# Turning a grouped convolution's results on VectorE instead of TensorE, with a new partition order of its input

## The chip, the core and the metric

The kernel runs on one core of one Trainium2 chip. The core has a matrix engine (TensorE, PE in the profile), a vector engine (VectorE, DVE), a scalar engine (ScalarE, ACT), GpSimd (POOL) and SyncE (SP). They run their own instruction streams and wait for each other by semaphores. A transfer is started by an instruction in the stream of one of the engines and is carried out by the core's 16 DMA engines. In this kernel nearly all transfers are started from SP.

The metric is the device time of one execution in microseconds. Before the change the median of three runs is 2969.51 us (2966.65 to 2975.18).

## What is computed

The input is 32 images of 14 x 14 pixels with 512 channels, float32. Two residual layers follow each other, each behind a group norm over 32 groups of 16 channels (`_gn`):

```python
def _L0_conv_ref(x, block_w, block_b, fc1_w, fc1_b, fc2_w, fc2_b, gammas):
    anchors = []
    for i in range(NUM_BLOCKS):                       # 18
        nx = gelu(einsum('bhwc,cd->bhwd', x, block_w[i]) + block_b[i])
        if i in TARGET_IDX:                           # 11, 14, 17
            t = TARGET_IDX.index(i)
            pooled = nx.mean(axis=(1, 2))
            h = gelu(pooled @ fc1_w[t] + fc1_b[t])
            logits = (h @ fc2_w[t] + fc2_b[t]).reshape(-1, A, C)
            gates = softmax(logits, axis=1)
            routed = einsum('bac,bahwc->bhwc', gates, stack(anchors))
            nx = nx + gammas[t] * routed
        x = nx
        if i in ANCHOR_IDX:                           # 1, 4, 9
            anchors.append(x)
    return x

def _L1_conv_ref(x, W):                               # 3 x 3, SAME, 32 groups
    return conv_general_dilated(x, W, ..., feature_group_count=32)

x = x + _L0_conv_ref(_gn(x), ...)
x = x + _L1_conv_ref(_gn(x), W)
```

The change concerns the second line, the 3 x 3 convolution in groups of 16 channels, and, on a small scale, how the input of the first one is brought in.

## The kernel before

**Blocks.** Channels lie on the 128 partitions, in four chunks, and pixels along the free dimension. A tile holds two images (392 pixels); sixteen tiles form eight pairs. One of the 18 blocks on a pair is a *step*: a 512 x 512 matrix product with seven half-size products instead of eight (`block`, L412; the products are line 431, the subtractions ahead of a step `pre_adds`, line 410, ScalarE saves intermediate results in line 464, VectorE adds in line 468, and the gelu is line 444 or 451). A product is a *tick*, so that a step has seven ticks. The steps of neighbouring pairs are interleaved in an order written out by hand, and ahead of step 15 of the last pair stands a *gap*, a step without products, in which other work of TensorE is put.

**The planner.** All other work is put at ticks. `at(tick, f)` places a call; `put(first, need, f)` places it at the first tick from `first` on at which VectorE ("dve") or ScalarE ("act") has `need` microseconds left of a budget (`ROOM`, by the tick's number within the step; `TAIL` behind the last step, `tend`); `hold` takes some of a budget away. `block` calls `run(tick)` behind each product, and that is the order in which the engines' streams, SP's too, receive their instructions. The streams are in order: a transfer whose buffer isn't free holds up everything that SP has behind it.

**Start of a pair.** `plan_start` begins LEAD ticks ahead of a pair's first step. `load_blocks` fetches 32 x 12 x 32 blocks of the transposed input (`xb`, line 256, from four SP instructions per tile and chunk) and the remaining eight pixels' part of all four chunks (`xr`), and VectorE turns them in 32 x 32 blocks (`turn_blocks`, lines 274 and 276). NIN = 4 such buffers are in use at a time.

**Gates.** After blocks 11, 14 and 17 the weights of the gate are loaded (line 517 for the first layer), then `gate_hidden` (`hps`, line 547), `gate_logits` (`lps`, line 563), a softmax, and the weighted sum of the anchors by VectorE and ScalarE (`gate_part`, `gate_add` in line 643, `gate_last`, `gate_base` in line 611). Behind the last block GpSimd adds the input to the result (`residual`, a transfer that accumulates).

**From layer one to layer two.** `plan_norm` computes the group norm's statistics, and `columns` writes the sum and its normed form into `xc` (lines 721, 731, 733) and from there to DRAM, in `x2d` (line 740). A row of `x2d` is one image column of one channel; columns 0 to 7 and 6 to 13 are the two halves `v` (KC = 8 columns each, of which SO = 7 are results), index `e` tells the plain sum from its normed form, and the last index runs over 8 images x 14 rows, NV = 112.

**Convolution.** Two pairs form a batch of eight images (NBAT = 4). A batch has 16 *units* of two groups of 16 channels each; four units (UC) make up one chunk of 128 channels. The partitions of a unit are the 16 channels and 8 columns of a group, so that the taps along a row become three 128 x 128 band matrices, one for each of the three rows of the filter. They are built once by VectorE (`load_taps`, `build_band`, lines 828 and 835, with `mask`), stored in DRAM and fetched again for each unit or kept. A unit goes through four calls:

1. `unit_load`: one SP instruction (line 858) brings both groups' rows, 448 KB; where the bands aren't kept another one (line 866) brings them.
2. `unit_taps`: twelve matmul instructions (line 879) into PSUM.
3. `unit_sum`: VectorE adds the result to the plain sum, in place (line 889).
4. `unit_out`: four transposes on TensorE (line 903, `tpo`) put images and rows on the partitions; two ScalarE copies (line 908) put them into the output tile `o` of 112 x 14 x 128; after the chunk's fourth unit ScalarE starts one output transfer of 784 KB (line 913).

`plan_unit` places these: the load some ticks ahead, no earlier than the unit five places back (NX = 5 buffers) has gone out; then the sum with 0.65 us of VectorE and `unit_out` with 0.9 us of ScalarE. Batches 0 and 1 have their 16 units beside the blocks of later pairs. Of batch 2 four units stand ahead of the gap, NGAP = 6 in the gap, and NLATE = 6 behind the last step (`tend`), where they fill TensorE while the last pair's gate and norm are computed. The 16 units of batch 3 come last of all, chunk by chunk as the norm's results arrive.

Of the kernel before, what the change touches and what calls it, by code (L numbers as in the profile page):

```python
# [19 lines left out]
def kernel(  # L20
# [53 lines left out]
    inpool = ctx.enter_context(tc.tile_pool(name="inpool", bufs=4))  # L74
# [59 lines left out]
    def run(tick):  # L134
# [23 lines left out]
        mask[:, 1 : GP + 1], ident.rearrange("p (i k) -> p k i", k=GP), AX.X, ALU.add  # L158
# [92 lines left out]
    def load_blocks(t, c):  # L251
# [8 lines left out]
        if c == 0:  # L260
            xr = d["xr"] = inpool.tile([P, NCK, TB], F32, tag="xr", name=f"xr_{t}", bufs=2)
            for q in range(P // TB):
                nc.sync.dma_start(xr[q * TB : (q + 1) * TB], cols[q, N - TB :])

    def turn_blocks(t, c):
# [9 lines left out]
        if cc == NH - 1:  # L275
            nc.vector.transpose(xq[:, :, N - TB :], d["xr"][:, h * NH : (h + 1) * NH])
            nc.sync.dma_start(xkeep[t][h], xq.rearrange("p c n -> p (c n)"))
# [60 lines left out]
    def plan_start(p):  # L338
# [3 lines left out]
        NIN = 4  # L342
# [4 lines left out]
        for j, (t, c) in enumerate(parts):  # L347
            at(t0 - LEAD - 8 if j < NIN else turned[j - NIN], load_blocks, t, c)
            turned.append(put(max(a, turned[j - NIN] + 5 if j >= NIN else 0), {"dve": 0.45 + c % NH * 0.15}, turn_blocks, t, c))
# [457 lines left out]
    def load_taps(c):  # L807
# [3 lines left out]
        for i in range(CG):  # L811
            nc.sync.dma_start(
                tw[i * KC : (i + 1) * KC], src[i].partition_broadcast(KC)
            )
# [4 lines left out]
    def build_band(g, dx):  # L819
# [3 lines left out]
        shape = [P, 3, CG, KC]  # L823
        if dx == 0:
# [5 lines left out]
            tw[:, :, dx, gl * CG : (gl + 1) * CG].unsqueeze(3).to_broadcast(shape),  # L830
            mask[:, dx : dx + KC].unsqueeze(1).unsqueeze(1).to_broadcast(shape),
# [4 lines left out]
        if dx == 2:  # L836
            nc.sync.dma_start(band[g // 2][:, g % 2], t[0].rearrange("p y o k -> p (y o k)"))
            del built[g]
# [15 lines left out]
    def unit_load(m, u):  # L854
# [3 lines left out]
        nc.sync.dma_start(  # L858
            xs.rearrange("r g e n -> r g (e n)"),
            x2d[m][c].rearrange("(g r) e v n -> r g (e v n)", r=P)[:, 2 * ul : 2 * ul + 2],  # L860
        )
# [30 lines left out]

    def unit_out(m, u):

        d = units.pop((m, u))
        c, ul = divmod(u, UC)
        if ul == 0:
            outs[m] = outpool.tile([NV, W, P], F32, tag="o", name=f"o_{m}_{c}")
        tp = aux(f"tpo_{m}_{u}")
        for g in range(2):  # L900
            for v in range(2):
                j = v * 2 + g
                nc.tensor.transpose(  # L903
                    tp[:NV, j * P : (j + 1) * P], d["xs"][:, g, 0, v * NV : (v + 1) * NV], ident
# [183 lines left out]
```

## Time and profile before

| | |
|---|---|
| median of the three runs | 2969.51 us |
| the profiled execution's own time | 2968.65 us |
| span of its profile, from the first to the last instruction | 2966.6 us |
| granted TensorE clock | 0.994 |
| matmuls of line 431, x<-t,s alone (the largest of its groups) | 2304 x 494 ns |
| transposes of results, tpo, line 903 | 256 instructions, 38.8 us busy |
| copies of them, line 908 on ScalarE | 128 x 348 ns, 37.8 us busy |
| sums, line 889 on VectorE | 64 x 616 ns, 39.3 us busy |
| bytes moved by transfers that SP starts (q1) | 448.79 MB |
| bytes moved by those that ScalarE starts (q10) | 13.65 MB |
| mean rate of all transfers over the span | 161 GB/s |

An instruction's mean is the time from its start to its end; TensorE overlaps successive instructions, so that the busy time of a group of matmuls is less than count times mean (256 transposes of 274 ns are 38.8 us busy, 152 ns each). "Busy" of an engine is the share of the span in which it executed something, and says nothing of who waited for whom. For that the page has the chain that ended last: from the last instruction back, at each step, to what released it, or to the instruction before it on its engine. A group's "idle before" is how long its engine stood idle just ahead of these instructions, with what ended most of that. SPq is SyncE's own sequencer, that is, the instructions that start transfers; the time of such an instruction is the time that SP is held, not that of the transfer.

The page also divides the span into 40 slices of 74 us. TensorE is 90% busy or more in all but the first and the last (8 and 6 tenths), its granted clock is at nine tenths or more in all but the last (8), and the transfers' share of the 16 DMA engines' time, between 3 and 7 tenths up to there, is 8 and 9 tenths in the last two slices.

### The profile page before, as it was taken

The page shows a single profiled execution, that of the slowest core. Times are in us where ns is not written, and L with a number is a line of the kernel's source. Part 1 is how long each engine was busy: PE and PEld are TensorE (multiplying, and loading weights), DVE is VectorE, ACT ScalarE, POOL GpSimd, SP SyncE. Part 2 cuts the span into 40 slices and gives each one's busy share as a digit, 9 for nine tenths or more (in the row PEclk, how much of TensorE's full clock was granted, in tenths as well). Part 3 has the DMA queues.
Part 4 walks back from the last instruction along what each step waited for, and adds up shares of the span by engine and source line. Part 5 has one row for each costly group of instructions (what it writes and reads, how often), then busy time and mean ns, then how long its engine had stood idle before and what let it go on. Part 6 is the DMA issues. An engine that isn't in the chain of part 4 may idle for free.

```text
span 2966.6 us, 31628 instructions
## 1 busy us (share of the span) xinstructions
PE 2926.8 (99%) x9889; PEld 1795.7 (61%) x9889; DVE 1764.8 (59%) x3393; ACT 1430.9 (48%) x3355; POOL 78.1 (3%) x60
## 2 busy tenths in 40 slices
PE   8999999999999999999999999999999999999996
PEld 5555555555556566666666666666666665656666
DVE  5887787755377454763547635576455753545663
ACT  4435445545455444554444544445445454544561
POOL 0000000000000000000000000000000000000010
PEclk9999999999999999999999999999999999999998
DMA  5554446733475346654566544665446653343689
GB/s 160 163 181 138 164 145 174 202 114 117 149 198 158 130 135 175 205 164 130 166 164 182 172 135 154 173 175 168 140 154 165 182 159 125 122 136 118 205 224 212
DMA packets 483017, 477.31 MB, mean 161 GB/s; under 512 B 247987, under 2 KB 310562, under 8 KB 482850
## 3 DMA queue, kind: packets, MB, share of 16 engines
q1 hardware_dynamic: 452450, 448.79, 49.4%
q0 software_dynamic: 4608, 12.85, 2.4%
q10 hardware_dynamic: 25792, 13.65, 1.8%
q8 instruction: 80, 1.31, 0.2%
q14 instruction: 87, 0.71, 0.1%
HBM read 393.41 MB, written 93.03 MB: 164 GB/s over the span
## 4 chain that ended last, share of the span: by engine, by line
PE 96%; DVE 1%; DMA 1%; SPq 1%; issue 0%; ACT 0%; DVEq 0%
PE x L431 50%; PE z L431 25%; PE y L431 13%; PE cps L879 5%; PE lps L563 1%; PE tpo L903 1%; PE hps L547 1%; SPq L740 0%; SPq L256 0%; SPq L851 0%; DMA x<-x2d 0%; PE warm L991 0%; DMA w<-in_L_conv_block_w_dram 0%; DMA xin<-in_x_dram 0%; DMA x2d<-xc 0%
## 5 line engine op out<-in xcount | busy, mean ns | idle before, releaser
L431 PE MATMUL x<-t,s 128*128 128x392 f32 x2304 | 809.6, 494 | 0.1
L444 ACT ACTIVATE o<-c,bias 128x392 f32<-128x392 f32 x720 | 440.3, 620 | 666.2 <-DVE c L468 662.5
L431 PEld LDWEIGHTS x<-t,s 128*128 128x128 f32 x2304 | 433.5, 190 | 301.9 <-issue 0.2
L468 DVE TENSOR_TENSOR c<-x,c 128x392 f32<-128x392 f32 x288 | 160.5, 565 | 491.3 <-PE x L431 417.3
L464 ACT COPY c<-x 128x392 f32<-128x392 f32 x576 | 278.2, 483 | 352.9 <-PE x L431 347.6
L431 PE MATMUL x<-t,w 128*128 128x392 f32 x1152 | 402.8, 492 | 1.0 <-DVE c L468 1.0
L431 PE MATMUL z<-t,s 128*128 128x392 f32 x1152 | 402.9, 492 | 0.0
L431 PE MATMUL y<-o,w 128*128 128x392 f32 x1088 | 380.9, 493 | 0.2 <-ACT o L444 0.2
L431 PE MATMUL z<-o,s 128*128 128x392 f32 x1088 | 380.6, 492 | 0.0
L431 PE MATMUL x<-o,w 128*128 128x392 f32 x1088 | 380.4, 492 | 0.0
L468 DVE TENSOR_TENSOR c<-y,c 128x392 f32<-128x392 f32 x288 | 162.4, 564 | 276.3 <-PE y L431 198.0
L431 PEld LDWEIGHTS x<-t,w 128*128 128x128 f32 x1152 | 218.8, 190 | 161.7 <-DVE c L468 1.6
L431 PEld LDWEIGHTS z<-t,s 128*128 128x128 f32 x1152 | 217.6, 190 | 154.5 <-DMA s<-skeep 0.3
L410 DVE TENSOR_TENSOR t<-o,o 128x784 f32<-128x784 f32 x272 | 264.0, 971 | 65.4 <-ACT o L444 63.5
L431 PEld LDWEIGHTS z<-o,s 128*128 128x128 f32 x1088 | 206.0, 190 | 148.9
L431 PEld LDWEIGHTS x<-o,w 128*128 128x128 f32 x1088 | 206.4, 190 | 147.8 <-DMA w<-in_L_conv_block_w_dram 0.7
L431 PEld LDWEIGHTS y<-o,w 128*128 128x128 f32 x1088 | 205.0, 190 | 146.2 <-ACT o L444 1.0
L410 DVE TENSOR_TENSOR t<-o,t 128x784 f32<-128x784 f32 x272 | 264.3, 972 | 4.7
L464 ACT COPY c<-z 128x392 f32<-128x392 f32 x288 | 139.2, 483 | 211.0 <-PE z L431 210.9
L468 DVE TENSOR_TENSOR c<-z,c 128x392 f32<-128x392 f32 x288 | 158.9, 563 | 109.7 <-PE z L431 108.5
L451 ACT ACTIVATE o<-c,bias 128x196 f32<-128x196 f32 x288 | 129.4, 450 | 91.3 <-DVE c L468 90.5
L444 ACT ACTIVATE o<-x,bias 128x392 f32<-128x392 f32 x240 | 137.3, 581 | 71.5 <-PE x L431 65.2
(109 smaller groups left out, 2014.3 us busy)
## 6 DMA issues: line engine op xcount, KB each, us to landing
w<-in_L_conv_block_w_dram SPq DMA_DIRECT2D x144, 1024.0 KB
s<-skeep SPq DMA_DIRECT2D x504, 256.0 KB
x2d<-xc SPq DMA_DIRECT2D x128, 224.0 KB
x<-x2d SPq DMA_DIRECT2D x64, 448.0 KB
skeep<-s SPq DMA_DIRECT2D x72, 256.0 KB
bw<-band SPq DMA_DIRECT2D x38, 384.0 KB
xkeep<-xt SPq DMA_DIRECT2D x32, 392.0 KB
o<-xkeep POOLq DMA_DIRECT2D x32, 392.0 KB, 7.4
```

Of the source, the lines that this page charges most:

```text
L410: nc.vector.tensor_tensor(t[j], i0, i1, ALU.subtract)
L431: nc.tensor.matmul(acc[d][:, :N], lhsT=lhsT[:, kk, d * P : (d + 1) * P], rhs=rhs[:, kk, :], start=first and kk == 0, stop=kk == NH - 1, sk ...
L444: nc.scalar.activation(o[:, d, :], srcs[d], AF.Gelu_apprx_tanh, bias=bias[:, r : r + 1])
L451: nc.scalar.activation(o[:, d, sl], srcs[d][:, sl], AF.Gelu_apprx_tanh, bias=bias[:, r : r + 1], accum_out=pooled[:, c, m : m + 1],)
L464: nc.scalar.copy(cs[d], acc[d][:, :N])
L468: nc.vector.tensor_tensor(cs[d], acc[d][:, :N], cs[d], ALU.add)
L547: nc.tensor.matmul(hps[:, :NB4], lhsT=w1[:, kk, :], rhs=box["pooled"][:, kk, :], start=(kk == 0), stop=(kk == NCK - 1),)
L563: nc.tensor.matmul(lps[:, m * NB4 : (m + 1) * NB4], lhsT=w2[:, m * P : (m + 1) * P], rhs=h, start=True, stop=True,)
L879: nc.tensor.matmul(pv[:, :, lo:hi], lhsT=d["bw"][:, g, dy], rhs=xv[:, :, lo + dy - 1 : hi + dy - 1], start=j == 0, stop=j == 2, skip_group ...
L903: nc.tensor.transpose(tp[:NV, j * P : (j + 1) * P], d["xs"][:, g, 0, v * NV : (v + 1) * NV], ident)
```

## The change

Input, bands and output of the convolution take another order, and with it another engine turns the results:

- **Partition order.** The partitions of a unit are (column, channel) instead of (channel, column): in `mask`, in the bands (`build_band`), and in `unit_load`, whose source is now rearranged. That takes two transfers of one group each in place of one of two. `x2d` itself stays as it was. `load_taps` fills its tile with eight transfers of 16 partitions instead of sixteen of 8.
- **Turning.** `unit_out` has two VectorE transposes in 32 x 32 blocks, one for each group, in place of four on TensorE and two copies on ScalarE. 32 partitions are two columns of 16 channels. A block takes 28 (TR) of the 112 positions and 4 more, which belong to the next block and aren't used; 8 blocks (of both halves) make up a group, 256 elements a partition. The output tile `o` has 32 positions x 4 pairs of columns on its partitions.
- **Output.** After the chunk's fourth unit 14 transfers go out, one for each image column, of 28 x 4 rows of 128 channels, started by SP; before, it was one, started by ScalarE.
- **Planner.** `unit_out` books 0.6 us of VectorE, possibly at the tick of the sum, and nothing of ScalarE; the budgets held for the units in the gap and behind the last step change accordingly. NGAP is 5 and NLATE 7, where they were 6 and 6.
- **Start of a pair.** `inpool` has three buffers instead of four, and NIN is 3; the remainder `xr` is loaded for two chunks at a time instead of four; LEAD is 42 instead of 35, the first loads start 6 ticks ahead of the turning instead of 8, and a later block is turned 4 ticks or more behind its load instead of 5.

```diff
--- before.py
+++ after.py
@@ -71,7 +71,7 @@
     fpool = ctx.enter_context(tc.tile_pool(name="fpool", bufs=1))
     qpool = ctx.enter_context(tc.tile_pool(name="qpool", bufs=38))
     tmp = ctx.enter_context(tc.tile_pool(name="tmp", bufs=6))
-    inpool = ctx.enter_context(tc.tile_pool(name="inpool", bufs=4))
+    inpool = ctx.enter_context(tc.tile_pool(name="inpool", bufs=3))
     outpool = ctx.enter_context(tc.tile_pool(name="outpool", bufs=2))
     cvpool = ctx.enter_context(tc.tile_pool(name="cvpool", bufs=2))
     small = ctx.enter_context(tc.tile_pool(name="small", bufs=2))
@@ -155,7 +155,7 @@
     mask = const.tile([P, GP + 2], F32, name="mask")
     nc.vector.memset(mask, 0.0)
     nc.vector.tensor_reduce(
-        mask[:, 1 : GP + 1], ident.rearrange("p (i k) -> p k i", k=GP), AX.X, ALU.add
+        mask[:, 1 : GP + 1], ident.rearrange("p (k i) -> p k i", k=GP), AX.X, ALU.add
     )
 
     mhalf = const.tile([P, NR], F32, name="mhalf")
@@ -257,10 +257,10 @@
                 xs[q * TB : (q + 1) * TB],
                 cols[q, : NTB * TB, c].rearrange("(n j) i -> j n i", j=TB),
             )
-        if c == 0:
-            xr = d["xr"] = inpool.tile([P, NCK, TB], F32, tag="xr", name=f"xr_{t}", bufs=2)
+        if c % NH == 0:
+            xr = d["xr", c // NH] = inpool.tile([P, NH, TB], F32, tag="xr", name=f"xr_{t}_{c}", bufs=2)
             for q in range(P // TB):
-                nc.sync.dma_start(xr[q * TB : (q + 1) * TB], cols[q, N - TB :])
+                nc.sync.dma_start(xr[q * TB : (q + 1) * TB], cols[q, N - TB :, c : c + NH])
 
     def turn_blocks(t, c):
         d = starts[t]
@@ -273,7 +273,7 @@
         xq = d["xq"][h]
         nc.vector.transpose(xq[:, cc, : NTB * TB], xs.rearrange("p n i -> p (n i)"))
         if cc == NH - 1:
-            nc.vector.transpose(xq[:, :, N - TB :], d["xr"][:, h * NH : (h + 1) * NH])
+            nc.vector.transpose(xq[:, :, N - TB :], d.pop(("xr", h)))
             nc.sync.dma_start(xkeep[t][h], xq.rearrange("p c n -> p (c n)"))
 
     xkeep = [
@@ -339,14 +339,14 @@
 
         t0 = NP7 * at_step[p, 0]
         parts = [(2 * p + n, c) for n in range(2) for c in range(NCK)]
-        NIN = 4
+        NIN = 3
         a = t0 - LEAD
         at(a - 30, copy_in, p)
         turned = []
         b = 0
         for j, (t, c) in enumerate(parts):
-            at(t0 - LEAD - 8 if j < NIN else turned[j - NIN], load_blocks, t, c)
-            turned.append(put(max(a, turned[j - NIN] + 5 if j >= NIN else 0), {"dve": 0.45 + c % NH * 0.15}, turn_blocks, t, c))
+            at(t0 - LEAD - 6 if j < NIN else turned[j - NIN], load_blocks, t, c)
+            turned.append(put(max(a, turned[j - NIN] + 4 if j >= NIN else 0), {"dve": 0.45 + c % NH * 0.15}, turn_blocks, t, c))
             a = turned[j]
         for j, (t, c) in enumerate(parts):
             b = max(b, put(turned[j // NH * NH + NH - 1], {"dve": 0.7}, stats_in, t, c))
@@ -808,10 +808,8 @@
 
         tw = outpool.tile([P, NTAP, P], F32, tag="o", name=f"tw_{c}")
         src = conv_w.rearrange("kh kw i d -> i (kh kw) d")[:, :, c * P : (c + 1) * P]
-        for i in range(CG):
-            nc.sync.dma_start(
-                tw[i * KC : (i + 1) * KC], src[i].partition_broadcast(KC)
-            )
+        for k in range(KC):
+            nc.sync.dma_start(tw[k * CG : (k + 1) * CG], src)
         taps[c] = tw
 
     built = {}
@@ -820,21 +818,21 @@
 
         tw = taps[g // GP].rearrange("p (y x) d -> p y x d", x=3)
         gl = g % GP
-        shape = [P, 3, CG, KC]
+        shape = [P, 3, KC, CG]
         if dx == 0:
             built[g] = cvpool.tile([P, 2] + shape[1:], F32, tag="x", name=f"bt_{g}", bufs=NX)
         t = [built[g][:, v] for v in range(2)]
         o = t[min(dx, 1)]
         nc.vector.tensor_tensor(
             o,
-            tw[:, :, dx, gl * CG : (gl + 1) * CG].unsqueeze(3).to_broadcast(shape),
-            mask[:, dx : dx + KC].unsqueeze(1).unsqueeze(1).to_broadcast(shape),
+            tw[:, :, dx, gl * CG : (gl + 1) * CG].unsqueeze(2).to_broadcast(shape),
+            mask[:, dx : dx + KC].unsqueeze(1).unsqueeze(3).to_broadcast(shape),
             ALU.mult,
         )
         if dx > 0:
             nc.vector.tensor_tensor(t[0], t[0], o, ALU.add)
         if dx == 2:
-            nc.sync.dma_start(band[g // 2][:, g % 2], t[0].rearrange("p y o k -> p (y o k)"))
+            nc.sync.dma_start(band[g // 2][:, g % 2], t[0].rearrange("p y k o -> p (y k o)"))
             del built[g]
 
     units = {}
@@ -855,10 +853,9 @@
 
         c, ul = divmod(u, UC)
         xs = cvpool.tile([P, 2, 2, 2 * NV], F32, tag="x", name=f"x_{m}_{u}", bufs=NX)
-        nc.sync.dma_start(
-            xs.rearrange("r g e n -> r g (e n)"),
-            x2d[m][c].rearrange("(g r) e v n -> r g (e v n)", r=P)[:, 2 * ul : 2 * ul + 2],
-        )
+        src = x2d[m][c].rearrange("(g i k) e v n -> g k i (e v n)", i=CG, k=KC)
+        for g in range(2):
+            nc.sync.dma_start(xs[:, g].rearrange("r e n -> r (e n)"), src[2 * ul + g])
         if u in bands:
             bw = bands[u] if m < NBAT - 1 else bands.pop(u)
         else:
@@ -890,31 +887,33 @@
             x2, x2, d["ps"][:, : 4 * NV].rearrange("p (g n) -> p g n", g=2)
         )
 
+    TR = 28
+    NR4 = NV // TR
+
     def unit_out(m, u):
+
 
         d = units.pop((m, u))
         c, ul = divmod(u, UC)
         if ul == 0:
-            outs[m] = outpool.tile([NV, W, P], F32, tag="o", name=f"o_{m}_{c}")
-        tp = aux(f"tpo_{m}_{u}")
+            outs[m] = outpool.tile([P, 2 * NR4, 2, P], F32, tag="o", name=f"o_{m}_{c}")
+        o = outs[m]
         for g in range(2):
-            for v in range(2):
-                j = v * 2 + g
-                nc.tensor.transpose(
-                    tp[:NV, j * P : (j + 1) * P], d["xs"][:, g, 0, v * NV : (v + 1) * NV], ident
-                )
-        for v in range(2):
-            src = tp[:NV, v * 2 * P : (v + 1) * 2 * P]
-            nc.scalar.copy(
-                outs[m][:, v * SO : (v + 1) * SO, ul * 2 * CG : (ul + 1) * 2 * CG],
-                src.rearrange("q (o l) -> q l o", l=KC)[:, v : v + SO],
-            )
-        if ul == UC - 1:
-            nc.scalar.dma_start(
-                out[m * BI : (m + 1) * BI, :, :, c * P : (c + 1) * P].rearrange(
-                    "b h w d -> (b h) w d"
-                ),
-                outs[m],
+            v = d["xs"][:, g].rearrange("r e n -> r (e n)")
+            nc.vector.transpose(
+                o[:, :, :, (ul * 2 + g) * CG : (ul * 2 + g + 1) * CG],
+                bass.AP(v.tensor, v.offset, [v.ap[0], [TR, 2 * NR4], [1, TB]]),
+            )
+        if ul < UC - 1:
+            return
+        for w in range(W):
+            v, l = divmod(w, SO)
+            q, j = divmod(l + v, 2)
+            nc.sync.dma_start(
+                out[m * BI : (m + 1) * BI, :, w, c * P : (c + 1) * P].rearrange(
+                    "b h d -> (b h) d"
+                ).rearrange("(n r) d -> r n d", r=TR),
+                o[q * TB : q * TB + TR, v * NR4 : (v + 1) * NR4, j],
             )
 
     done = []
@@ -931,7 +930,7 @@
             a += 1
         at(a, unit_taps, m, u)
         b = put(a + 1, {"dve": 0.65}, unit_sum, m, u)
-        b = put(b + 1, {"act": 0.9}, unit_out, m, u)
+        b = put(b, {"dve": 0.6}, unit_out, m, u)
         done.append((a, b))
 
     def plan_batch(m):
@@ -947,14 +946,12 @@
             if m == NBAT - 2:
                 for j in range(NGAP):
                     tk = NP7 * at_step[NPAIR - 1, GAP] + NP7 * j // NGAP
-                    hold("dve", tk + 1, -0.65)
-                    hold("act", tk + 2, -0.9)
+                    hold("dve", tk + 1, -0.66)
                     if j >= NBW:
                         at(tk - 10, load_bands, (early + j,))
                     plan_unit(m, early + j, tk, 10, j >= NBW)
                 for j in range(NLATE):
-                    left["dve"][tend + 1 + j] += 0.65
-                    left["act"][tend + 2 + j] += 0.9
+                    hold("dve", tend + 1 + j, -0.66)
                     at(tend - 12 + j, load_bands, (early + NGAP + j,))
                     plan_unit(m, early + NGAP + j, tend + j, 12, True)
         else:
@@ -997,8 +994,8 @@
     pre_adds(0, "0")
 
 
-    NGAP, NLATE = 6, 6
-    LEAD = 35
+    NGAP, NLATE = 5, 7
+    LEAD = 42
     for k in range(len(steps)):
         p, i = steps[k]
         if i == GAP:
@@ -1016,16 +1013,11 @@
             for tk, us in enumerate((0.8, 0.0, 1.5, 1.5, 0.5, 0.0, 0.0)):
                 left["act"][NP7 * k + tk] = us
     for j in range(NLATE):
-        left["dve"][tend + 1 + j] = TAIL["dve"] - 0.65
-        left["act"][tend + 2 + j] = TAIL["act"] - 1.05
-    for j in range(NLATE):
-        left["dve"][tend + 1 + j] = TAIL["dve"] - 0.65
-        left["act"][tend + 2 + j] = TAIL["act"] - 0.9
+        hold("dve", tend + 1 + j, 0.66)
     left["act"][tend] = left["act"][tend + 1] = 0.0
     for j in range(NGAP):
         tk = NP7 * at_step[NPAIR - 1, GAP] + NP7 * j // NGAP
-        hold("dve", tk + 1, 0.65)
-        hold("act", tk + 2, 0.9)
+        hold("dve", tk + 1, 0.66)
     gated = {}
     for p in range(NPAIR):
         plan_differences(p)
```

## Prediction

> **What bounds the kernel now.** First the page's busy shares and the chain that ended last, then the groups by shape.
>
> ```profile
> span 2966.6 us, 31628 instructions
> PE 2926.8 (99%) x9889; PEld 1795.7 (61%) x9889; DVE 1764.8 (59%) x3393; ACT 1430.9 (48%) x3355; POOL 78.1 (3%) x60
> PE 96%; DVE 1%; DMA 1%; SPq 1%; issue 0%; ACT 0%; DVEq 0%
> PE x L431 50%; PE z L431 25%; PE y L431 13%; PE cps L879 5%; PE lps L563 1%; PE tpo L903 1%; PE hps L547 1%; SPq L740 0%; SPq L256 0%; SPq L851 0%; DMA x<-x2d 0%; PE warm L991 0%; DMA w<-in_L_conv_block_w_dram 0%; DMA xin<-in_x_dram 0%; DMA x2d<-xc 0%
> ```
>
> TensorE is the bound, and the transposes of line 903 lie in its chain: what is taken out of its queue shortens the run, as long as nothing else is late. The chain in order of time gives the price of one conv unit, in the gap before step 15 of the last pair:
>
> ```profile
> 2794.22 2.17 PE cps L879 x12
> 2796.38 0.44 PE tpo L903 x4
> 2796.82 2.17 PE cps L879 x12
> 2798.98 0.44 PE tpo L903 x4
> ```
>
> Columns: start, duration. A unit costs TensorE 2.17 for its taps and 0.44 for four transposes, 2.60 in all. The end, from the same view, is another matter:
>
> ```profile
> 2865.88 1.54 PE hps L547 x8
> 2867.41 7.27 PE cps L879 x24
> ...
> 2904.63 5.26 DMA x2d<-xc
> ...
> 2914.85 6.55 DMA x<-x2d
> ...
> 2955.77 2.18 PE cps L879 x12
> 2957.97 0.63 DVE x L889
> ```
>
> The last product ends at 2863.05 (timeline), so 103.5 us follow it: the last gate, the norm of the last pair, and the conv units of the last batch, of which the first starts at 2913.56. Until there VectorE and transfers set the pace; from there TensorE, at 2.60 a unit.
>
> **The body: a gain.** Before, 42 units stand ahead of the last product (16+16+4+6 in the gap); after, 41 (five in the gap, seven late). 42 x 2.60 = 109.2 becomes 41 x 2.17 = 89.0: **-20.2 us**, and the last product ends at 2842.8.
>
> What comes in its place on VectorE:
>
> ```profile
> L274 DVE STREAM_TRANSPOSE xt<-xb 128x384 f32<-128x384 f32 x56 | 30.6, 564 | 0.0
> L276 DVE STREAM_TRANSPOSE xt<-xr 128x64 f32<-128x64 f32 x28 | 6.9, 245 | 1.0
> ```
>
> Two durations (564 ns for 384 elements, 245 for 64) give 181 ns plus 1.0 ns an element. A new transpose has 256 elements: 437 ns, between those rows as bounds; 128 of them add 56 us, 0.87 a unit. VectorE waits 417, 198 and 108 us for TensorE's x, y and z in its adds at line 468, so they fit; uncovered, the whole 56 us would show. The planner books 0.60 for 0.87: 0 to 5 us lost, I take 0. ScalarE loses 37.8 us of copies; nobody waited long for it.
>
> In the gap VectorE is tighter. From 2790.7 it has eight gate adds (0.50 from start to start), six gate parts (0.35), five sums (0.54), two of line 611 (0.97), four transposes (0.44) and two pre-adds (0.97): 14.4, ready at 2805.1. TensorE wants the second pre-add after five units, the gate's 0.8 and two products: 2788.4 + 10.9 + 0.8 + 5.3 = 2805.4. It just holds; 0 to 2 us.
>
> Lines costed at nothing: the mask and band layouts (same counts and elements); eight tap loads for sixteen (VectorE waited 7.5 us for them, TensorE 1.0 at 57.7: a gain of 0 to 1); three buffers for four in the pair's start, issued earlier by the larger LEAD, with eight small remainder loads for four, at some 0.5 us of SP each, far ahead of their need. The nine output bursts in the body stand in SP's queue before weight and sum loads. Those go out about seven ticks (18 us) before their use, and a burst holds SP 5.3 us: 0 to 3, I take 0.
>
> **SP's queue: the price.** Issue durations on SP (min/median/max ns):
>
> ```profile
> L256 SPq DMA_DIRECT2D xb<-xcol x224: 303/468/2281, 133.6 to 2314.6; - x112
> L369 SPq DMA_DIRECT2D w<-in_L_conv_block_w_dram x144: 383/384/864, 4.0 to 2825.3; - x144
> L740 SPq DMA_DIRECT2D x2d<-xc x128: 512/667/3787, 514.5 to 2926.3; - x128
> L858 SPq DMA_DIRECT2D x<-x2d x64: 359/426/2939, 930.7 to 2948.0; - x64
> ```
>
> Where both sides have the same dimensions (256, 369) an issue takes 0.3 to 0.47; where they differ (740) 0.67. An output is now 14 equal-sided DMAs: 0.38 each, **5.3 us** a burst, bounds 0.30 and 0.67. A unit load becomes two DMAs with unequal sides: 2 x 0.65 = 1.3 for 0.43. The Trainium skill (DMA: Bandwidth & Descriptors, Issuing engines are not separate DMA queues) calls the issuing time usually small beside the DMA; by that the move from ACT to SP is free. The row decides: 5.3 us of issue for 802,816 bytes that ACT issued in 0.58, standing in order ahead of loads.
>
> **Engines per load.** The same page (Why a DMA increments its semaphore by 16 and not by 1) says that a DMA spreads over the largest count up to 16 that divides the slowest dimension of both sides. That speaks against this change: a unit load's source is now 8 x 16 x 448, so 8 engines. The trace has such a case, the old tap loads of 8 partitions, almost alone:
>
> ```profile
> 46.50:54.50 8.00, 8.00 (x26) 4.59 (x25) 0.46 (x2) 2.56 (x5) 0.00 (x0) 1.00 0.48 57
> 2850.00:2860.00 10.00, 10.00 (x37) 6.10 (x37) 4.32 (x15) 6.44 (x21) 1.76 (x1) 1.00 0.99 301
> ```
>
> The last two columns are the DMA engines' share and GB/s: 0.48 when eight-row loads queue, 0.99 otherwise. It agrees with the rule. A unit's 256 packets of 1792 bytes take 74 ns each in the trace: 1.18 us over 16 engines, 2.37 over 8. An output's 1568 packets of 512 bytes (27 ns) over 14 engines: 3.0.
>
> **The end, step by step.**
> 1. Gate. Its weights (line 517) queue behind SP's work, with engines full (0.99). Ahead of them are now one output burst (3.0) and four unit loads at 1.2 more each, less one load: +6.5; the engines are half idle at the start of the stretch, so I take +5 (0 to 9). The gate's first matmul: 2.8 + 5 after the last product, 2850.6.
> 2. Norm. Line 731's second block ended 37.6 later before; one sum (0.5) and a 1.6 us wait for TensorE go: 35.5. The late units' transposes stand behind it in VectorE's order.
> 3. Then statistics (2.7) and a unit's two transposes (0.9) free a buffer; two late loads (2.6), x2d (1.3) and a burst of 14 (5.3) go ahead of the first load of the last batch (1.3), which lands 3.2 + 1.2 later: 53.3 after the gate, where it was 47.7. First taps at 2903.9, TensorE's clock low after idling, as the page shows after its idle stretches now.
> 4. Sixteen units. TensorE alone needs 8.7 per four; the lower eight engines 4 x 2.37 + 3.0 = 12.5; SP 4 x 1.3 + 5.3 = 10.5 and waits. Engines: 15 loads 35.6, four bursts 12, one x2d 2 = 49.6 to the last load's landing. Then taps 2.2, sum 0.6, transposes 0.9, the last 14 outputs 5.3, the final write some 2: 60 in all, where 53.0 was. End at 2963.9.
>
> The profiled run took 2968.65 for its span of 2966.6, so 2.05 more: **2966 us**, against 2968.65; the median shown is 2969.51. The gain of 20 is spent in the end stage: 5 at the gate, 4 net in front of the last batch, 7 in it, one late unit.
>
> **Rivals.**
> - *The end keeps its pace* (0.32). If unit loads still use 16 engines, or bursts hide beside the taps, the end costs from nothing extra (103.5 + 2.2 - 7 for sixteen units: span 2941.5) to SP's order alone (some 15 more). **2952**, 2942 to 2960. For it: a load needs only 426 ns on SP and DMA share falls to 0.38 in the last 17 us. Against: the 0.48 above.
> - *SP decides, and it is slower* (0.23). Seven bursts, 98 DMAs, lie on the end's chain in one in-order queue; with engines full an issue stretches (the fourteen x2d from 2884.34 took 21.55, 1.54 each). At 0.60 instead of 0.38 this costs 21.6: **2987**. It decides from 0.53. Against: the equal-sided rows stay below 0.47.
>
> **How the numbers follow.** The forecast's case has 0.45, its own range 2955 to 2977. Below 0.3% either way (about 9 us around 2969.5) a measurement can't tell from no change: of the 0.45, 0.14 falls below, 0.20 within, 0.11 above. Faster 0.14 + 0.32 = 0.46; same 0.20; slower 0.11 + 0.23 = 0.34. Range 2944 to 2986.
>
> **What would show it.** The body: the last product near 2843 and no transposes on TensorE. VectorE's transposes near 437 ns. Gate matmul 7 to 9 us after the last product. In the last batch taps come in fours with stalls on x<-x2d, DMA share near 0.7 at best, SP issuing output at 0.38. It is wrong if the last product ends well after 2843 (stalls on VectorE in the body), if unit loads fill 16 engines, or if taps follow each other at 2.17 to the end.

## The result, and the profile after

The changed kernel takes 3012.45 us (median of 4 runs, 3009.82 to 3015.85) beside 2970.78 us for the kernel before on the same chip. It is slower: the ratio is 1.0141, 95% interval 1.0122 to 1.0160. The forecast of 2966 us, and its range up to 2986, were wrong. The profiled execution took 3009.82 us.

The page of the changed kernel, busy shares and the chain that ended last:

```profile
span 3008.1 us, 31503 instructions
PE 2912.1 (97%) x9633; PEld 1782.7 (59%) x9633; DVE 1810.0 (60%) x3521; ACT 1394.0 (46%) x3227; POOL 78.2 (3%) x60
PE 94%; DMA 2%; SPq 2%; DVE 1%; issue 0%; ACT 0%; DVEq 0%
```

TensorE works 15 us less than before and the span is 41.5 us longer. Transfers and SP now hold 4% of the chain, about 120 us, where they held 2%. Where they stand is seen in TensorE's own timeline behind the last product (start, duration, line; in brackets the idle time before it and what ended it):

```profile
2840.93 2.80 PE L431 MATMUL x<-t,w 128*128 128x392 f32 x8
2868.76 1.84 PE L547 MATMUL hps<-pool,w 128*128 128x4 f32 x8 [25.04 <-DMA w<-in_L_conv_fc_w_dram]
...
2926.95 10.50 PE L876 MATMUL cps<-x,bq 128*128 128x224 f32 x48 [7.55 <-DMA x<-x2d]
2945.78 7.93 PE L876 MATMUL cps<-x,bq 128*128 128x224 f32 x30 [8.33 <-DMA x<-x2d]
...
2961.14 12.86 PE L876 MATMUL cps<-x,bq 128*128 128x224 f32 x60 [5.56 <-DMA x<-x2d]
2979.70 9.12 PE L876 MATMUL cps<-x,bq 128*128 128x224 f32 x36 [5.71 <-DMA x<-x2d]
2993.28 4.61 PE L876 MATMUL cps<-x,bq 128*128 128x224 f32 x12 [4.47 <-DMA x<-x2d]
```

The same three points in the kernel before, the last product, the gate's first matmul and the first taps of the last batch:

```profile
2860.25 2.80 PE L431 MATMUL x<-t,w 128*128 128x392 f32 x8
2865.88 1.54 PE L547 MATMUL hps<-pool,w 128*128 128x4 f32 x8 [2.83 <-DMA w<-in_L_conv_fc_w_dram]
2913.56 4.30 PE L879 MATMUL cps<-x,bq 128*128 128x224 f32 x12 [8.42 <-DMA x<-x2d]
```

The last product ends at 2843.7, 19.3 us earlier than before. Then the gate waits 25.0 us for its weights (2.8 before), and in the last batch the taps come in groups of three to five units with 4 to 8 us of waiting for `x` ahead of each. From this view of each run come the four stages that the rest of the text uses, all in us (the last batch's taps begin at 2926.95; the 24 taps at 2913.39 are the two late units that had to wait for a buffer):

| stage | before | forecast | after |
|---|---|---|---|
| last product ends | 2863.1 | 2842.8 | 2843.7 |
| wait until the gate's first matmul | 2.8 | 7.8 | 25.0 |
| from there to the last batch's first taps | 47.7 | 53.3 | 58.2 |
| from there to the end | 53.0 | 60.0 | 81.2 |

**Ahead of the gate.** SP in the changed kernel (start, time from the first instruction of the group to the end of its last, count), from the output burst two steps before the end to the gate's weights of line 517:

```profile
2816.95 7.79 SPq L912 DMA_DIRECT2D out_dram<-o  x14
...
2840.69 5.83 SPq L740 DMA_DIRECT2D x2d<-xc  x2
2846.56 11.71 SPq L849 DMA_DIRECT2D bq<-band  x4
2858.37 5.88 SPq L740 DMA_DIRECT2D x2d<-xc  x4
2864.30 1.25 SPq L517 DMA_DIRECT2D w<-in_L_conv_fc_w_dram  x1
```

The same stretch of the kernel before:

```profile
2848.15 2.46 SPq L740 DMA_DIRECT2D x2d<-xc  x2
2850.70 5.28 SPq L851 DMA_DIRECT2D bq<-band  x3
2856.08 5.36 SPq L740 DMA_DIRECT2D x2d<-xc  x4
2861.49 1.19 SPq L517 DMA_DIRECT2D w<-in_L_conv_fc_w_dram  x1
```

Relative to the end of the last product SP came to the weights 1.6 us early before and comes 20.6 us late now. The groups in between hold it longer although they are nearly the same: 11.71 us for four band loads. In the waits of SP these lines have 0.4 us at most: it is the instructions themselves that take long, while the 16 engines are full with the transfers ahead of them. Ten us of it in the changed kernel (window, its length, busy time of PE, PEld, DVE, ACT and POOL with counts, TensorE's clock, the DMA engines' share, GB/s):

```profile
2846.00:2856.00 10.00, 0.00 (x0) 0.00 (x0) 1.77 (x7) 0.00 (x0) 1.73 (x2) 0.60 1.05 222
```

**In the last batch.** SP of the changed kernel between two bursts and the next:

```profile
2945.70 11.49 SPq L912 DMA_DIRECT2D out_dram<-o  x14
2957.29 6.46 SPq L858 DMA_DIRECT2D x<-x2d  x10
2966.48 9.13 SPq L912 DMA_DIRECT2D out_dram<-o  x14
2975.70 3.83 SPq L858 DMA_DIRECT2D x<-x2d  x6
2979.63 9.61 SPq L912 DMA_DIRECT2D out_dram<-o  x14
2989.34 1.22 SPq L858 DMA_DIRECT2D x<-x2d  x2
```

and what SP waited for behind 2905, ahead of line 912 (us in total, times, longest):

```profile
SPq L912 <- DMA x<-x2d: 13.5, 15, 1.7
SPq L912 <- DVE o L903: 10.9, 2, 8.7
```

(Of the second line 8.7 us are the very last burst, which waits for the last unit's result.) Loads and bursts take turns on SP. An output needs no data from `x`. It waits for a load because of how this program signals landings: in the trace's record of the instructions each of SP's 1773 transfers has one of eight semaphores, taken in turn, and starts only when the transfer before on the same semaphore, here the one eight places ahead, has landed. The few transfers that ScalarE starts take theirs from the same eight. A burst behind six to ten such loads (two to a unit) thus lasts until most of them are in, and the next loads stand behind the burst.

### The profile page after: what moved, and what is told of

Same layout as the page of the kernel before. It is cut to its first block, busy times and chain, and to the rows that moved or that the text cites. A ratio compares the mean times of both kernels' runs of the same rounds, so it can differ in the third digit from the quotient of the medians.

```text
span 3008.1 us, 31503 instructions
## 1 busy us (share of the span) xinstructions
PE 2912.1 (97%) x9633; PEld 1782.7 (59%) x9633; DVE 1810.0 (60%) x3521; ACT 1394.0 (46%) x3227; POOL 78.2 (3%) x60
## 4 chain that ended last, share of the span: by engine, by line
PE 94%; DMA 2%; SPq 2%; DVE 1%; issue 0%; ACT 0%; DVEq 0%
PE x L431 50%; PE z L431 25%; PE y L431 13%; PE cps L876 4%; DMA x<-x2d 1%; PE lps L563 1%; SPq L912 1%; PE hps L547 1%; DMA w<-in_L_conv_fc_w_dram 1%; SPq L849 1%; SPq L740 1%; SPq L858 0%; PE warm L988 0%; PE tpi L301 0%; DVE o L621 0%
```

## The experiments

Each run's gate wait and last batch are read from the same timelines, of one execution that can lie up to 4 us off the median. The stretch ahead of the gate is the same in the changed kernel and in out_act, and they wait 25.0 and 26.2 us: differences of about 1 us between stages say nothing. The kernels with whole loads and before_split exchange channels and columns of the convolution's input, and those called no_residual leave an addition out; they show what a time is made of and are no replacement. Two theories: **L**, the unit load, spread over 8 of 16 engines ("half-width"), is what costs; **S**, the bursts in SP's queue are. The median of before that the runs were compared with was 2967.2 to 2968.8 us.

| run | us | ratio to before, 95% interval | gate wait | last batch |
|---|---|---|---|---|
| changed kernel | 3012.45 | 1.0141 (1.0122, 1.0160) | 25.0 | 81.2 |
| loads_whole | 2978.85 | 1.0036 (1.0023, 1.0049) | 19.7 | 61.3 |
| out_act | 2993.17 | 1.0085 (1.0068, 1.0102) | 26.2 | 66.3 |
| gate_early | 2995.09 | 1.0089 (1.0074, 1.0104) | 0.2 | 81.3 |
| before_split | 3003.89 | 1.0119 (1.0104, 1.0134) | 19.1 | 65.0 |
| no_residual | 3003.49 | 1.0124 (1.0107, 1.0141) | 17.9 | 83.9 |
| burst_behind | 3004.38 | 1.0127 (1.0112, 1.0142) | 26.7 | 83.2 |
| rows16 | 2990.03 | 1.0081 (1.0066, 1.0096) | 21.4 | 66.0 |
| burst_pool | 3006.60 | 1.0135 (1.0117, 1.0153) | 20.2 | 81.5 |
| whole_no_residual | 2970.88 | 1.0010 (1.0003, 1.0017) | 11.9 | 60.2 |
| whole_burst_pool | 2974.14 | 1.0019 (1.0011, 1.0027) | 13.5 | 59.9 |
| end_act | 2978.06 | 1.0036 (1.0023, 1.0049) | 0 | 72.2 |
| end_act_whole | 2950.54 | 0.9944 (0.9929, 0.9959) | 0 | 52.1 |
| end_act_late5 | 2969.25 | 1.0006 (0.9997, 1.0015) | 0 | 71.0 |
| rows16_end_act | 2963.75 | 0.9982 (0.9976, 0.9989) | 0 | |
| rows16_late5 | 2965.29 | 0.9989 (0.9981, 0.9998) | 0 | 56.5 |
| rows16_pool | 2963.03 | 0.9980 (0.9973, 0.9987) | 0 | |

In rows16_end_act and rows16_pool the taps of the last batch follow the late units' without a gap, so that their start can't be read.

### Loads and bursts, one at a time

loads_whole:

```diff
-        src = x2d[m][c].rearrange("(g i k) e v n -> g k i (e v n)", i=CG, k=KC)
-        for g in range(2):
-            nc.sync.dma_start(xs[:, g].rearrange("r e n -> r (e n)"), src[2 * ul + g])
+        nc.sync.dma_start(
+            xs.rearrange("r g e n -> r g (e n)"),
+            x2d[m][c].rearrange("(g r) e v n -> r g (e v n)", r=P)[:, 2 * ul : 2 * ul + 2],
+        )
```

> The changed kernel with the unit load of before (one DMA of 128 rows for both groups); channels and columns of the convolution's input are then exchanged, so its results are others. Theory L (the load spread over 8 of 16 engines is what costs, at the gate and in the last batch): both stages recover, gate matmul within 10 us of the last product, last batch 55 to 60 us, 2958 to 2975. Theory S (bursts of output DMAs standing ahead of loads in SP's queue cost): only issue time comes back, about 0.9 us for each of 16 units, 2990 to 3003.

33.6 us came back, 20 of them in the last batch: 4 us above L's range, since the gate still waits 19.7 us where L said at most 10.

before_split has the opposite edit in the kernel before.

> The kernel before with only the unit load of the changed one (two DMAs, source 8 x 16 x 448); channels and columns of the convolution's input are then exchanged, so its results are others. Theory L: slower by 15 to 30 us, 2985 to 3000, with TensorE waiting for x in the last batch. Theory S: the loads stay hidden behind TensorE's 2.60 us a unit, since nothing stands between them in SP's queue, 2970 to 2979.

It is 35 us slower than before, more than L said; the bursts alone can't be the cause. TensorE's waits in it:

```profile
PE hps L547 <- DMA w<-in_L_conv_fc_w_dram: 19.1, 1, 19.1
PE cps L878 <- DMA x<-x2d: 17.3, 5, 9.4
```

The load alone, with no burst on SP and TensorE still at 2.60 us a unit, brings both waits.

out_act:

```diff
-            nc.sync.dma_start(
+            (nc.scalar if m == NBAT - 1 else nc.sync).dma_start(
```

> The changed kernel with the four output bursts of the last batch started by ScalarE instead of SP. Theory S: the last batch falls from 94.7 us to 55 to 62, the gate stays 25 us late, 2970 to 2982. Theory L: loads still need 2.4 us each on 8 engines and nothing is gained but issue time, last batch 85 or more, 2998 to 3012.

(Its 94.7 us count from 2913.39, with the two late units.) 19.3 us came back, between the two. Two bursts of the third batch are still ahead of the loads on SP; once they are through, ten units follow in 26.3 us, 2.6 each, not far from the 2.37 us that the forecast gave a load on 8 engines.

burst_behind leaves the bursts on SP, two ticks later (the line that places them):

```diff
+        if u % UC == UC - 1:
+            at(b + 2, unit_store, m, u)
```

> The changed kernel with every output burst placed two ticks later, on SP still, so that two or three loads of the next units stand ahead of it instead of behind it. If the order on SP alone costs: last batch 10 us or more shorter, 2990 to 3003. If the bound is that SP has eight DMAs under way at most and each burst waits for loads to land, whatever the order: no gain, 3007 to 3015.

8 us, between both expectations, and none of it in the last batch: its first taps came 52.8 us after the gate instead of 58.2, and the batch itself took 83.2 us. Whichever stands first on SP, each waits for the other to land.

### Eight engines or two instructions?

Whole loads differ in two things from the changed kernel's. rows16 keeps two DMAs per unit, of the same size and on SP, and changes only the order of the rows so that the slowest dimension is 16. It pays with two stores of 64 partitions for one in line 740; taps and turned results take the new order too, with one VectorE copy more per chunk of taps (not shown).

```diff
-        src = x2d[m][c].rearrange("(g i k) e v n -> g k i (e v n)", i=CG, k=KC)
+        src = x2d[m][c].rearrange("(g i k a) e v n -> g (k a) i (e v n)", a=2, k=KC, i=CG // 2)
...
+            for a in range(2):
+                nc.sync.dma_start(
+                    x2d[m][c].rearrange("(q k a) e v n -> a q k e v n", k=KC, a=2)[
+                        a, :, :, e, v, j * PV : (j + 1) * PV
+                    ],
+                    xc[a::2, w0 : w0 + KC],
+                )
```

> The changed kernel with x2d's rows, and with them the order of channels within a group, arranged so that a unit load's source is 16 x 8 x 448 instead of 8 x 16 x 448; still two DMAs of the same size for a unit. For it each store of x2d becomes two of 64 partitions, and taps and turned results take the new channel order. Theory L (8 engines instead of 16): close to the run with whole loads, last batch 60 to 66 us, 2976 to 2988. Rival (two instructions instead of one, and their longer issue, are what cost): last batch 75 us or more, 2998 to 3014.

22.4 us came back, 15 of them in the last batch: 2 us above L's range and 8 below the rival's. Ten of these transfers, five units' loads, queue in both kernels; the windows in which they run, changed kernel first (columns as above, the last two are the DMA engines' share and GB/s):

```profile
2959.00:2966.00 7.00, 4.86 (x19) 4.75 (x20) 0.94 (x2) 0.00 (x0) 0.00 (x0) 0.64 0.50 175
```

and rows16:

```profile
2946.00:2952.00 6.00, 3.84 (x21) 3.85 (x22) 2.00 (x5) 0.00 (x0) 0.00 (x0) 1.00 0.98 247
```

0.50 against 0.98, as if half of the engines were idle while loads of 8 x 16 x 448 queue; the rate rises less, from 175 to 247 GB/s. The rule that the forecast took from the Trainium skill (DMA: Bandwidth & Descriptors, Why a DMA increments its semaphore by 16 and not by 1), the largest count up to 16 that divides both slowest dimensions, fits both shares.

### The wait at the gate

no_residual leaves out GpSimd's four accumulating transfers of the last pair.

```diff
-                at(tick, residual, n, h, p)
+            if p < NPAIR - 1:
+                at(tick, residual, n, h, p)
```

> The changed kernel without the last pair's residual, that is, GpSimd's four accumulating transfers ahead of the norm (the input of the last four images is then not added). Theory R (once the gate's weights are late, they also stand behind these transfers, whose packets take 131 us of engine time, 8 us over 16 engines): the wait at the gate falls from 25 us to 15 to 19, 2999 to 3006. Rival: SP is held only by what stands ahead in its own queue; the wait stays at 22 us or more, 3008 to 3013.

The wait fell by 7.1 us, as theory R said. These transfers start when the last product ends, in the changed kernel 20 us ahead of the weights (2864.30):

```profile
2843.25 0.90 POOL L707 DMA_DIRECT2D o<-xkeep  x1 [1.40 <-DVE o L611]
```

Before, the weights went out just ahead of them.

Three more runs take the rest apart. whole_no_residual joins the two edits shown:

> The changed kernel with whole loads (one DMA of 128 rows for both groups; channels and columns of the convolution's input exchanged) and without the last pair's residual (its input is not added). If the parts add, 2.8 us for what was there before and 8 for the burst: the gate waits 10 to 13 us, where whole loads with the residual waited 19.7; 2968 to 2974. If the residual costs only on top of half-width loads, 17 to 20 us and 2976 to 2981.

burst_pool starts one burst, the one at 2816.95, from GpSimd:

```diff
+        eng = nc.gpsimd if m == NBAT - 2 and c == 1 else nc.sync
...
-            nc.sync.dma_start(
+            eng.dma_start(
```

> The changed kernel with only the output burst ahead of the end (third batch, second chunk) started by GpSimd instead of SP. If the parts add (2.8, loads 8, residual 7), the gate waits 16 to 20 us instead of 25, and the whole is 5 to 9 us faster, 3003 to 3008. If the transfers of the burst crowd the engines whoever starts them: 23 us or more, 3010 to 3014.

and whole_burst_pool has whole loads besides:

> As the run before with whole loads (channels and columns of the convolution's input exchanged): neither half-width loads nor the burst on SP stand ahead of the gate's weights. If nothing else delays them, the gate waits 2 to 6 us, as before the change, since the weights are again ahead of the residual; 2960 to 2968. If the residual is met all the same, 9 to 12 us.

The first came out as said (11.9 us), the second almost (20.2), the third not: it waited 13.5 us where 2 to 6 were expected, or 9 to 12 with the residual in the way. Its streams show why: it met the residual all the same. SP:

```profile
2842.13 3.00 SPq L517 DMA_DIRECT2D w<-in_L_conv_fc_w_dram  x1
```

GpSimd, first in that run, then in the kernel before:

```profile
2839.47 1.87 POOL L707 DMA_DIRECT2D o<-xkeep  x2 [1.45 <-ACT o L451]
```

```profile
2862.56 1.80 POOL L707 DMA_DIRECT2D o<-xkeep  x2 [1.39 <-DMA x2d<-xc]
```

Before, the weights started 1.1 us ahead of the residual (2861.49 and 2862.56); here 2.7 us behind. Pairs of runs that differ in one thing agree on the parts: half-width loads 5.3, 6.0 and 6.7 us (25.0 to 19.7, 17.9 to 11.9, 20.2 to 13.5), the burst on SP 4.8 and 6.2 (25.0 to 20.2, 19.7 to 13.5), the residual 7.1 and 7.8 (25.0 to 17.9, 19.7 to 11.9). With the 2.8 us of before they make some 22 of the 25; the remaining 3 weren't separated (the burst's transfers themselves and one band load more are left as candidates).

gate_early puts the weights ahead of all this:

```diff
-            at(NP7 * k + 4, load_gates, k)
+            at(NP7 * (k - 1) + 1 if k == len(steps) - 1 else NP7 * k + 4, load_gates, k)
```

> The changed kernel with the last gate's weights loaded one step earlier, so that they stand ahead of the late band loads, unit loads and the x2d stores. If the wait of TensorE of 25 us at the gate is lost time on the path: gate matmul within 3 us of the last product, 2988 to 2998. Rival: the norm behind it waits for the same full queue (stores of x2d, loads of late units), so the time comes back later and less than 6 us is gained, 3006 to 3014.

17.4 us of 25, inside the first expectation. The rest comes back at once. SP's stores of `x2d`, and TensorE behind them:

```profile
2866.54 26.60 SPq L740 DMA_DIRECT2D x2d<-xc  x20
```

```profile
2898.37 6.36 PE L876 MATMUL cps<-x,bq 128*128 128x224 f32 x24 [13.59 <-DMA x<-x2d]
```

The stores of the last two pairs keep SP until 2893, though the gate is early, at 1.3 us a store; the norm's third block (line 731) ends at 2886.2, and no run separates the two. The loads behind these stores are what TensorE waits for next.

### Towards a kernel that is faster

end_act has the gate weights early and all six bursts behind the last product on ScalarE:

```diff
+        late = m == NBAT - 1 or m == NBAT - 2 and c >= NCK // 2
+        eng = nc.scalar if late else nc.sync
...
-            nc.sync.dma_start(
+            eng.dma_start(
```

> The changed kernel with two edits together: the gate weights one step earlier, and the six output bursts behind the last product (two of the third batch, four of the last) started by ScalarE. If both act on one chain, SP's queue from the late stores of x2d to the first loads of the last batch, the bursts' removal also shortens the way to the first taps: no wait at the gate, first taps of the last batch near 2902, 50 us behind them, 2950 to 2960. If the two gains only add, 2974 to 2979.

2978.06 us, in the range of the second case: the gains only add. end_act_whole is the same with whole loads:

> As the run with both edits, but with unit loads as before (one DMA of 128 rows for both groups; channels and columns of the convolution's input exchanged, so its results are others). If loads over 8 engines still bind when nothing stands ahead of them, 10 to 20 us below that run; if TensorE's 2.17 us a unit and the norm bind by then, within 5 us of it.

2950.54 us, 27.5 us less where 10 to 20 were expected: with the six late bursts off SP, the half-width load and its second instruction are the bound. end_act_late5 has five late units, and the burst ahead of the end on GpSimd as in burst_pool:

```diff
-    NGAP, NLATE = 5, 7
+    NGAP, NLATE = 5, 5
```

> As the run with both edits, with five units instead of seven behind the last product (two more among the blocks) and the output burst that goes out two steps before the end started by GpSimd. Two units of 2.17 us go into the body, two loads of 2.4 us and their issues leave the stretch ahead of the last batch, and SP loses a burst of 6 to 8 us ahead of it: 4 to 10 us below the run with both edits. If the norm alone sets the first taps, no gain, or up to 4 us slower.

8.8 us less than end_act, inside the expected range. rows16_end_act joins the edits of rows16 and end_act.

> As rows16, with the gate weights one step earlier and the six bursts behind the last product started by ScalarE. Theory L: close to the same with whole loads (2950.5), up to 12 us more for two DMAs a load and twice the stores: 2950 to 2962. Rival: at the run with both edits and loads over 8 engines, 2972 to 2980.

2963.75 us, 2 us above the range of L, 48.7 us less than the changed kernel, and a little below the kernel before: 0.9982 of it, an interval clear of 1, though the 0.2% are less than the 0.3% that the prediction counted as a change. Two more steps from there, rows16_late5 with the edits of end_act_late5, and rows16_pool with that of burst_pool:

> As rows16_end_act, with five late units instead of seven and the burst ahead of the end started by GpSimd, which brought 9 us with loads over 8 engines. With loads over 16 the two loads saved are worth half as much: 3 to 9 us below rows16_end_act.

> The best version so far (loads over 16 engines, gate weights early, six late bursts from ScalarE), with the burst ahead of the end started by GpSimd. SP comes 6 to 8 us earlier to the stores of x2d, but these fill the engines (share above 1 from 2830 to 2880 in the profile of that version) and the burst's transfers stay: 2 to 6 us below it, 2958 to 2962. If SP's issue is the bound, 6 to 9 us below.

2965.29 us, 1.5 us more instead of 3 to 9 less, and 2963.03 us, 0.7 less instead of 2 to 6. In rows16_end_act SP and the engines are full of stores ahead of the last batch; SP, then two windows of ten us:

```profile
2861.06 34.62 SPq L741 DMA_DIRECT2D x2d<-xc  x40
```

```profile
2860.00:2870.00 10.00, 4.08 (x19) 3.76 (x19) 9.45 (x39) 8.97 (x22) 2.04 (x2) 0.54 1.19 207
2870.00:2880.00 10.00, 2.59 (x11) 2.32 (x11) 9.27 (x39) 1.05 (x2) 2.12 (x2) 0.50 1.15 144
```

The engines' share is above 1 at only 144 to 207 GB/s; the packets of `x2d` have 224 bytes.

The forty stores begin earlier in the other two but don't end earlier. In rows16_late5:

```profile
2855.66 46.00 SPq L741 DMA_DIRECT2D x2d<-xc  x40
```

What the stores waited for while these forty went out, in rows16_end_act (2860 to 2896), rows16_late5 (2855 to 2902) and rows16_pool (2857 to 2897), each the longest entry of SP's waits:

```profile
SPq L741 <- DMA out_dram<-o: 5.2, 2, 3.4
SPq L741 <- DMA out_dram<-o: 13.3, 3, 11.6
SPq L741 <- DMA out_dram<-o: 9.8, 2, 7.9
```

The outputs are those that ScalarE starts. They come from the same eight semaphores as SP's transfers, so that moving a burst to ScalarE doesn't free SP of it: in the wait of 11.6 us a store stood until an output, started at 2884.54 on its semaphore, had landed at 2886.2, and that burst had waited for VectorE's last transposes (2881.5). What the stores gain at their start they lose here. In end_act_late5, where 9 us came, no store among the twenty (2862 to 2891) waited for an output. No run takes this wait away, so that its worth isn't shown.

## Why the prediction was wrong

- **The body** was right: -19.3 us instead of -20.2. The gap cost 1.0 us, a wait for the gate's weights, of the 0 to 2 allowed. VectorE's transposes and SP's starts were near their estimates (437, 380 and 650 ns):

```profile
L903 DVE STREAM_TRANSPOSE o<-x 128x256 f32<-128x256 f32 x128 | 48.7, 421 | 1.2
```

```profile
L912 SPq DMA_DIRECT2D out_dram<-o x224: 319/400/3749, 1092.0 to 3005.1; - x112
L858 SPq DMA_DIRECT2D x<-x2d x128: 574/590/1620, 929.4 to 2990.0; - x128
```

- **Step 1 failed, "I take +5".** It was +22.2. The sum of 6.5 us had engine time for the burst and the loads and was cut to 5 for engines thought half idle. The runs show half-width loads at 5 to 7 us and the burst at 5 to 6, some 11 together; that the weights, once late, fall behind the residual (7 to 8 us) wasn't in it at all. GpSimd's four transfers were in the trace of before, 1.1 us behind the weights, and no step asked what starts next if SP is late.
- **Step 2 held:** the second block of line 731 ended 35.1 us behind the gate's first matmul (at 2903.87), where 35.5 were forecast.
- **Step 3** was near: 58.2 us instead of 53.3 (its terms, as listed, add to 54.0, and those of step 4 to 60.6). The burst ahead of the first load held SP for 9.5 us instead of the 5.3 that 14 starts take.
- **Step 4 failed: 60 us became 81.2.** The rate on 8 engines was near (2.6 us a unit in out_act, forecast 2.37). The mistake was to take the larger of engine time and SP time for four units, 12.5 us, as if the two ran side by side. They take turns: from the burst at 2932.67 to that at 2999.38 are four rounds of 16.7 us on average, with a share of the engines of 0.52 to 0.61 where 0.7 was forecast. To the last unit's taps 66.3 us passed for 49.6; the rest is the tail, 14.8 us for 11; 2.4 of this difference are these taps at a low clock.
- **The rivals.** "The end keeps its pace" had the highest single chance of the others (0.32) and is refuted by the share of 0.50. "SP decides, and it is slower" (0.23) was right that the bursts in SP's in-order queue decide, and wrong in how: not a longer start (0.40 us at the median, where 0.60 was named) but waits between them, so that a burst with six to ten loads ahead held SP for 8.9 to 11.5 us, 0.64 to 0.82 an output, past the point of 0.53 from which this rival decides. Its 2987 us were still 25 too low; it left step 1 as it was, which is 17 of them.
- The forecast took its parts apart and priced each by durations of undisturbed transfers. The split load, with half the engines and a second instruction, is worth 35 us in the kernel before (before_split) and 34 here (loads_whole); 22 came back with both instructions kept and twice the stores (rows16). It was booked, bursts included, at 5 at the gate and 7 in the last batch.

## What to carry to other kernels

A queue that receives instructions in order, with a fixed number of transfers under way, must be priced in turns and landings, not by how long it takes to start a transfer: ask for each which landing it waits for (here the transfer eight places ahead, ScalarE's counted in), and what stands behind. When a load's access pattern is rearranged, work out how many engines its slowest dimension lets it use before asking how long it takes to start. And when something on the path becomes late, look in the trace for what it now collides with: here a residual that used to come just behind.

## What the runs showed of the hardware

- A start of a transfer on SP can stand for long though the landing it waits for is past: single ones of lines 740 and 849 took up to 5.2 and 8.9 us ahead of the gate in the changed kernel, while the engines' share was 1.0.
- TensorE's granted clock fell with the waits: 0.63 to 0.82 in the rounds of the last batch, where the kernel before had 0.89 to 1.00. The last unit's taps took 4.61 us, where the same line of the timeline before has 2.33.
- The Trainium skill (DMA: Bandwidth & Descriptors, Issuing engines are not separate DMA queues) says that starting transfers from several engines saves only the time of starting them. In out_act that was no small thing: 56 outputs of 0.40 us, 22 us, moved to ScalarE, and 19.3 us came back. How much of these is starts and how much the waits between them wasn't separated: in the changed kernel the four bursts held SP for 36 us.
